# Order of the weight loads and place of one job's one-hots in the expert part of a transformer block

## The chip, the cores and the metric

The kernel runs on one core of one Trainium2 chip. The metric is device time in microseconds of one execution. The engines are named as in the profile: PE (TensorE, with PEld its weight loads), DVE (VectorE), ACT (ScalarE), POOL (GpSimd) and SP (SyncE, used here only to issue DMAs). Each engine takes its instructions in program order. A DMA is issued by an instruction on SP, ACT or POOL, and moves its data on the core's 16 DMA engines.

## The reference, cut to what matters

Sixteen sequences of 256 tokens with 256 features pass an attention layer with 16 heads. Then each of 8 experts chooses 512 of all 4096 tokens by their gate, and a two-layer network of that expert is added to those tokens.

```python
tok = x.reshape(-1, d)                      # after attention, 4096 x 256
gate = jax.nn.softmax(tok @ Wgate.T, axis=-1)
vals, idx = jax.lax.top_k(gate.T, k_cap)    # 512 tokens for each of 8 experts
idx_flat = idx.T.reshape(-1)
w = vals.T
g = _ln(tok[idx_flat], mlp_g, mlp_b).reshape(k_cap, E, d)
y = jnp.einsum('ked,ehd->keh', g, fc1s) + b1s       # hidden 1024
y = jax.nn.gelu(y, approximate=True)
y = jnp.einsum('keh,edh->ked', y, fc2s) + b2s
y = y * w[..., None]
tok = tok.at[idx_flat].add(y.reshape(-1, d))
```

## The kernel before

**Two ways of ordering.** The sequences are worked through first, under a plan written out by hand: each step of each part (a group of the projection, a quarter of the heads, a tail) has a number for its place, `at` collects the steps with their numbers, and one loop at L1064 issues them in the order of the numbers. A number is a place in the order and no time of this run. The tail of a sequence (`Tail`, two halves of 128 tokens each) projects the attention's result, adds the input (`residual`, which also writes the tokens to `out`), normalises (`power`, `apply`, which writes rows to `xn_dram`), transposes (`transposes`, `evict`) and computes the gate logits (`gate`, `gate_evict`). In the lists called `tail` the numbers stand in the order of these eight steps, `evict` sixth.

**Routing.** A first routing (`Routing`) chooses half of each expert's tokens, 256, from the first 30 tiles of 128 tokens, while the last sequence is still worked on; a second one chooses the other half from all 32 tiles. The second routing is cut into small steps that run inside the expert jobs (`second_routing`, L1074).

**Jobs.** There are 16 expert jobs (`Job`): eight of the first routing, numbered 0 to 7, and eight of the second, 8 to 15. A job
- loads its weights (`load`, L866): `w1` for the first layer (256 rows of 4 KB, L869), `w2` for the second (1024 rows of 1 KB, L871), and the bias `b2` (L873), all on SP;
- turns the routing into a list of tokens: `gives` (3 DVE operations, L879 and L887), one-hot matrices for each tile of tokens (`onehot`, L897, one DVE operation each), and a small matmul for each of these (`list_matmul`, L906); `take` brings the result to SBUF;
- fetches the chosen rows from `xn_dram` by two indirect DMAs of 128 rows on POOL (`gather`, L925) and transposes them (`transposes` L934, `evict` L941);
- runs the first layer (`up` L953 on PE, `gelu` L960 on ACT, eight of each) and the second (`down` L969, two halves of 128 tokens);
- finishes each half on DVE (`finish` L975, L976) and adds it to `out` by an indirect DMA on POOL (`scatter` L979). A scatter waits until the one before it has landed.

**Order in the jobs.** Job 0 and the lists of jobs 0 and 1 are part of the plan. Jobs 1 to 15 run in a loop (L1099) of 16 slots each: a slot is one `up` and `gelu` (slots 0 to 7) or a quarter of a `down` (slots 8 to 15). In job k, the list of job k+1 is multiplied and its rows are gathered at slot 5 (slot 7 in job 7), and they are transposed at slot 14. The one-hots of job k+2 are made a few at a time from slot 6 on (`lay_out`, `parts`), and at the end of job k job k+2's `load` is issued. For job 2, whose `load` follows the plan directly, `gives` and 18 one-hots come after the whole plan and the remaining 12 in the first slots of job 1.

**Buffers.** The tiles `v`, `oT` and `kT` of the attention have two buffers each and serve the jobs too: `w1` lies in `v`, `w2` in `oT`, the one-hots in `kT`. So `w1` of job k+2 can be written when job k's last `up` has read its `w1`, and `w2` when its last `down` has read its `w2`. SP issues in order: a load that must wait holds up those behind it. The one-hots of job 2 lie where those of job 0 lay.

The gates of the last two tiles of tokens also pass between: `Gates.shift` and `divide` (DVE, L718 and L725) and `exp` (ACT, L722) are issued in the first slots of job 1, and `parts` (POOL, L737) after them. ACT's gelu and exp use different tables, so a table is loaded at each change.

Of the kernel before, what the change touches and what calls it, by code (L numbers as in the profile page):

```python
# [9 lines left out]
F32 = mybir.dt.float32  # L10
# [8 lines left out]
P = 128  # L19
B, N, D = 16, 256, 256  # L20
# [5 lines left out]
NT = NTOK // P  # L26
# [3 lines left out]
FC = DD // P  # L30
# [13 lines left out]
def kernel(  # L44
# [14 lines left out]
    nc = tc.nc  # L59
# [20 lines left out]
    def rsqrt(dst, src):  # L80
# [99 lines left out]
        tail=((75.94, 79.63, 83.54, 87.30, 84.99, 86.37, 88.80, 89.54), (90.54, 94.23, 95.33, 101.91, 95.74, 99.41, 105.55, 106.29)),  # L180
# [71 lines left out]
    END = {  # L252
        13: dict(
            tail=((785.465, 790.273, 798.692, 815.100, 809.231, 833.838, 858.249, 860.611), (801.111, 811.928, 832.334, 851.976, 852.521, 857.274, 860.648, 863.953)),
        ),
        14: dict(
            quad={
                (0, 0): (778.689, 786.219, 823.152),
                (0, 0, 0): (779.682, 781.429, 786.791, 815.299, 818.486),
                (0, 0, 1): (785.912, 785.925, 792.535, 808.580, 817.952),  # L260
# [23 lines left out]
            tail=((862.946, 865.847, 868.980, 875.067, 865.880, 866.612, 872.508, 873.385), (858.831, 861.745, 877.140, 877.177, 862.888, 865.191, 867.264, 869.065)),  # L284
# [43 lines left out]
            tail=((961.580, 961.705, 961.951, 972.971, 962.994, 969.038, 969.773, 970.133), (961.977, 963.425, 970.214, 973.543, 969.153, 973.476, 975.274, 976.692)),  # L328
# [45 lines left out]
    if True:  # L374
        attw = ctx.enter_context(tc.tile_pool(name="attw", bufs=1))
        seq = ctx.enter_context(tc.tile_pool(name="seq", bufs=2))
# [368 lines left out]
        class Routing:  # L745
# [46 lines left out]
            def step(self, n):  # L792

                old, self.cand = self.cand, bit.tile([P, 1], I32, tag="cand", name="cand")
                nc.vector.scalar_tensor_tensor(
                    self.cand, self.dropped, (1 << n) >> 1, old,
                    ALU.bitwise_or, ALU.bitwise_xor,
                )
# [62 lines left out]
        class Job:  # L861
# [2 lines left out]
                self.oh = None  # L864

            def load(self):  # L866
                e = self.e
                self.w1 = seq.tile([P, DC, DD], F32, tag="v", name="w1")
                nc.sync.dma_start(self.w1, fc1T[e].rearrange("(c p) f -> p c f", p=P))  # L869
                self.w2 = seq.tile([P, FC, D], F32, tag="oT", name="w2")  # L870
                nc.sync.dma_start(self.w2, fc2T[e].rearrange("(f p) d -> p f d", p=P))  # L871
                self.b2 = moe.tile([P, D], F32, tag="b2", bufs=3, name="b2")
                nc.sync.dma_start(self.b2, b2s[:, bass.ts(e, D)].to_broadcast([P, D]))  # L873

# [113 lines left out]
        def at(places, *steps):  # L988
            plan.extend((p, len(plan) + n, f) for n, (p, f) in enumerate(zip(places, steps)))
# [60 lines left out]
        jobs = [Job(e, r, n) for r, n in ((first, n1), (second, NT)) for e in range(E)]  # L1050
# [10 lines left out]
        for i in range(KL):  # L1061
            at(DOWN[i], partial(jobs[0].down, i), partial(jobs[0].finish, i))
            at([SCATTER + i * 0.1], partial(jobs[0].scatter, i))
        for _, _, step in sorted(plan, key=lambda s: s[:2]):  # L1064
            step()

# [19 lines left out]
        def lay_out(job):  # L1086

            job.gives()
            for a in list(range(0, 18, 2)) + list(range(18, NT, 3)):
                yield  # L1090
                job.onehot(a, a + (2 if a < 18 else 3))
# [1 line left out]
        rest = second_routing()  # L1093
        last = len(jobs) // 2 - 2
        jobs[2].load()
        parts = lay_out(jobs[2])
        for _ in range(10):
            next(parts)
        for k in range(1, len(jobs)):  # L1099
            a = jobs[k]  # L1100
            new = jobs[k + 1] if k + 1 < len(jobs) else None
# [2 lines left out]
            for s in range(SLOTS):  # L1104
# [17 lines left out]
                if far and k != last and s > LIST_AT:  # L1122
                    if s == LIST_AT + 1:
                        parts = lay_out(far)
# [62 lines left out]
```

## Time and profile before

| | us |
|---|---|
| median of three runs | 1217.5 (1215.92 to 1219.42) |
| the profiled execution, its own time | 1216.65 |
| span of the profiled execution, first to last instruction | 1214.6 |
| PE busy | 1171.7 (96%) |
| DVE busy | 764.5 (63%) |
| ACT busy | 618.2 (51%) |
| POOL busy | 591.0 (49%) |
| issue to landing, median: `w1` and `w2` (1 MB each) | 5.3 and 5.4 |
| issue to landing, median: gather and scatter (128 KB each) | 3.3 and 3.9 |

The profile is taken from one execution, and its microseconds count from the first instruction. A busy time is that of an engine with an instruction in hand, so a high share says which engine to look at first and not that it wastes nothing. The page cuts the span into 40 slices of 30.4 us and gives the busy share of each in tenths. A row of the timeline has the start, the length, engine, source line and operation, the tiles written and read, the number of merged instructions, and in brackets how long the engine stood idle before it and what it then waited for. The lines of the kernel are those in this row (L934 is line 934).

### The profile page before, as it was taken

The numbers are of one execution on the slowest core, as the hardware profiler recorded it, in microseconds if no ns is written. First come the engines' busy times: TensorE is split into PE (matmuls) and PEld (weight loads), VectorE is DVE, ScalarE is ACT, GpSimd is POOL, SyncE is SP. The second block draws the span as 40 slices with busy tenths as digits, with TensorE's granted clock in tenths as the row PEclk, the third lists the DMA queues.
The fourth block names the chain that finished last, engine by engine and source line by source line (L and its number), as shares of the span: only waits on it lengthen the run. The fifth ranks groups of instructions, "written<-read, shape, count | busy, mean of one in ns | idle before, by whom it ended". The sixth has DMA issues, their size and how long they took to land. (4 is left out here: it accounts for less than half of the span.)

```text
span 1214.6 us, 19466 instructions
## 1 busy us (share of the span) xinstructions
PE 1171.7 (96%) x6784; PEld 813.2 (67%) x6784; DVE 764.5 (63%) x2244; ACT 618.2 (51%) x1701; POOL 591.0 (49%) x818
## 2 busy tenths in 40 slices
PE   6999999999999999999999999999978999999996
PEld 3556666666575766666666757667645788888885
DVE  7656665756665666666675666565587477864541
ACT  2655555555555555555555556656563233233331
POOL 4654555545455565455554545554564233333332
PEclk9999999999999999999999999999998999999999
DMA  5000000000000000000000000000200556665661
GB/s 183 1 1 5 22 8 20 9 18 14 14 14 14 27 2 26 5 22 10 18 10 18 14 14 19 9 19 13 97 0 2 176 154 178 182 182 164 165 179 23
DMA packets 46738, 62.40 MB, mean 51 GB/s; under 512 B 3888, under 2 KB 39984, under 8 KB 46640
## 3 DMA queue, kind: packets, MB, share of 16 engines
q1 hardware_dynamic: 39808, 52.70, 13.1%
q0 software_dynamic: 6144, 8.39, 3.8%
q8 instruction: 54, 0.88, 0.3%
q14 instruction: 44, 0.36, 0.1%
q10 hardware_dynamic: 688, 0.06, 0.0%
HBM read 48.56 MB, written 12.58 MB: 50 GB/s over the span
## 5 line engine op out<-in xcount | busy, mean ns | idle before, releaser
L608 POOL TENSOR_SCALAR pr<-pr,sums 128x256 f32<-128x256 f32 x512 | 238.7, 484 | 274.9 <-DVE sums L604 258.3
L506 PE MATMUL pm<-wq,hT 128*128 128x512 f32 x768 | 354.3, 600 | 5.5 <-DMA wq<-in_wqkvT 3.4
L597 ACT ACTIVATE pr<-sc,nmax 128x256 f32<-128x256 f32 x512 | 236.4, 476 | 161.7 <-DVE nmax L588 147.2
L82 POOL TENSOR_TENSOR ss<-ss,neghalf 128x8 f32<-128x8 f32 x128 | 210.4, 1648 | 97.1 <-DVE ss L527 93.4
L506 PEld LDWEIGHTS pm<-wq,hT 128*128 128x128 f32 x768 | 137.1, 191 | 148.0 <-issue 136.6
L588 DVE TENSOR_REDUCE nmax<-sc 128x2 f32<-128x512 f32 x256 | 164.7, 682 | 44.6 <-PE sc L581 44.4
L523 DVE TENSOR_REDUCE ss<-sq 128x8 f32<-128x512 f32 x128 | 87.4, 683 | 106.0 <-ACT sq L519 105.8
L617 PEld LDWEIGHTS pp<-ident,pr 128*128 128x128 f32 x1024 | 120.0, 144 | 35.0 <-issue 20.4
L617 PE MATMUL pp<-ident,pr 128*128 128x128 f32 x1024 | 140.0, 277 | 3.3 <-ACT pr L597 2.5
L635 PE MATMUL po<-prT,v 128*64 128x256 f32 x1024 | 139.4, 395 | 0.7 <-ACT oT L645 0.7
L581 PE MATMUL sc<-kT,qT 64*128 64x256 f32 x1024 | 130.2, 392 | 0.0
L519 ACT ACTIVATE sq<-pm 128x512 f32<-128x512 f32 x128 | 77.1, 602 | 90.4 <-PE pm L506 88.7
L659 PE MATMUL pw<-wo,oT 128*128 128x256 f32 x512 | 118.5, 384 | 0.0
L953 PE MATMUL ph<-xT,w 128*128 128x256 f32 x512 | 118.3, 384 | 0.0
L581 PEld LDWEIGHTS sc<-kT,qT 64*128 64x128 f32 x1024 | 94.2, 187 | 34.7 <-issue 24.0
L969 PE MATMUL py<-w,hid 128*128 128x256 f32 x512 | 117.4, 382 | 0.0
L979 POOL DMA_INDIRECT out<-y,idx x32 | 51.4, 1605 | 124.2 <-DVE y L976 59.9
L597 ACT ACTIVATION_READ_ACCUMULATOR pr<-sc,nmax 128x1 f32 x512 | 105.8, 207 | 0.0
L659 PEld LDWEIGHTS pw<-wo,oT 128*128 128x128 f32 x512 | 95.7, 192 | 13.0 <-issue 0.8
L625 DVE COPY prT<-pp 128x512 f32<-128x512 f32 x112 | 76.9, 687 | 43.6 <-PE pp L617 42.7
L953 PEld LDWEIGHTS ph<-xT,w 128*128 128x128 f32 x512 | 94.9, 190 | 13.4 <-ACT xT L941 0.2
L969 PEld LDWEIGHTS py<-w,hid 128*128 128x128 f32 x512 | 94.9, 190 | 13.1
(118 smaller groups left out, 1267.0 us busy)
## 6 DMA issues: line engine op xcount, KB each, us to landing
w<-in_fc1T SPq DMA_DIRECT2D x16, 1024.0 KB, 5.3
w<-in_fc2T SPq DMA_DIRECT2D x16, 1024.0 KB, 5.4
xs<-in_x SPq DMA_DIRECT2D x16, 256.0 KB, 2.7
out<-tok SPq DMA_DIRECT2D x32, 128.0 KB, 1.7
xn_dram<-tn SPq DMA_DIRECT2D x32, 128.0 KB, 1.7
wq<-in_wqkvT SPq DMA_DIRECT2D x6, 512.0 KB, 8.5
b<-in_b2s SPq DMA_DIRECT2D x16, 128.0 KB, 5.3
wo<-in_woutT SPq DMA_DIRECT2D x1, 1024.0 KB, 10.2
```

The source lines that it names most:

```text
L82: nc.gpsimd.tensor_tensor(dst, src, neghalf[:, : src.shape[1]], ALU.pow)
L506: nc.tensor.matmul(self.pm, hTs[self.b][:, c, bass.ts(self.t, P)], wq[:, c, bass.ts(self.g, GW)], start=(c == 0), stop=(c == DC - 1),)
L523: nc.vector.tensor_reduce(self.ss[:, 0, :], self.sq.rearrange("p (h d) -> p h d", d=HD), AX.X, ALU.add,)
L581: nc.tensor.matmul(self.sc[i, j][:, t, :], qTs[self.b][rows, hp, bass.ts(t, P)], kTs[self.b][rows, hp, :], start=True, stop=True,)
L588: nc.vector.tensor_reduce(self.nmax[i, j], self.sc[i, j], AX.X, ALU.max, negate=True)
L597: nc.scalar.activation(self.pr[i, j][:, t, :], self.sc[i, j][:, t, :], AF.Exp, bias=self.nmax[i, j][:, t : t + 1], scale=1.0, accum_out=se ...
L608: nc.gpsimd.tensor_scalar(self.pr[i, j][:, t, :], self.pr[i, j][:, t, :], self.sums[i][:, 1, j, t : t + 1], 1.0, ALU.mult, ALU.mult,)
L617: nc.tensor.transpose(self.pp[i, j][:, c, bass.ts(t, P)], self.pr[i, j][:, t, bass.ts(c, P)], ident,)
L635: nc.tensor.matmul(self.po[j * HD : (j + 1) * HD, i, :], vs[self.b][:, c, bass.ts(4 * self.d + 2 * i + j, HD)], self.prT[i, j][:, c, :], s ...
L659: nc.tensor.matmul(self.pw, oTs[self.b][:, hp, bass.ts(self.t, P)], wo[:, hp, :], start=(hp == 0), stop=(hp == HP - 1),)
L953: nc.tensor.matmul(self.ph[f], self.w1[:, c, bass.ts(f, P)], self.xT[:, c, :], start=(c == 0), stop=(c == DC - 1),)
L969: nc.tensor.matmul(self.py[i], self.hid[:, f, bass.ts(i, P)], self.w2[:, f, :], start=(f == 0), stop=(f == FC - 1),)
```

## The change

Two things are changed. In `load`, `w2` is allocated and requested before `w1`. And for job 2, `gives` and all 30 one-hots are put into the plan at the place of the `evict` of the last sequence's first tail (the smaller sixth number of the two in `END[15]["tail"]`, 969.038, behind that `evict` as it was entered earlier); `parts` is empty until job 1 begins those of job 3.

```diff
             def load(self):
                 e = self.e
+                self.w2 = seq.tile([P, FC, D], F32, tag="oT", name="w2")
+                nc.sync.dma_start(self.w2, fc2T[e].rearrange("(f p) d -> p f d", p=P))
                 self.w1 = seq.tile([P, DC, DD], F32, tag="v", name="w1")
                 nc.sync.dma_start(self.w1, fc1T[e].rearrange("(c p) f -> p c f", p=P))
-                self.w2 = seq.tile([P, FC, D], F32, tag="oT", name="w2")
-                nc.sync.dma_start(self.w2, fc2T[e].rearrange("(f p) d -> p f d", p=P))
                 self.b2 = moe.tile([P, D], F32, tag="b2", bufs=3, name="b2")
                 nc.sync.dma_start(self.b2, b2s[:, bass.ts(e, D)].to_broadcast([P, D]))
...
             at(DOWN[i], partial(jobs[0].down, i), partial(jobs[0].finish, i))
             at([SCATTER + i * 0.1], partial(jobs[0].scatter, i))
+        at([min(t[5] for t in END[B - 1]["tail"])] * 2, jobs[2].gives,
+           partial(jobs[2].onehot, 0, NT))
         for _, _, step in sorted(plan, key=lambda s: s[:2]):
             step()
...
         jobs[2].load()
-        parts = lay_out(jobs[2])
-        for _ in range(10):
-            next(parts)
+        parts = iter(())
         for k in range(1, len(jobs)):
```

## The prediction, made before the changed kernel was run

> **What bounds the kernel now.** I read the page's slices first, then busy time by stage, then TensorE's own timeline through the expert jobs, then the DMA issues of one job.
>
> ```profile
> PE   6999999999999999999999999999978999999996
> DMA  5000000000000000000000000000200556665661
> q1 hardware_dynamic: 39808, 52.70, 13.1%
> ```
>
> TensorE (PE) is the bound almost everywhere; DMA is idle until the expert jobs, and there it is busy 60% of the time. The change only touches these jobs (from about 950 us) and the last tail before them. By stage (columns: stretch, its length, busy us and instructions of PE, weight loads, DVE, ACT, POOL, clock, DMA share, GB/s):
>
> ```profile
> 967.20:985.50 18.30, 17.38 (x103) 14.41 (x102) 14.24 (x77) 7.26 (x13) 8.12 (x10) 1.00 0.56 155
> 985.50:1080.20 94.70, 94.56 (x624) 80.70 (x623) 72.05 (x366) 28.84 (x60) 31.30 (x24) 1.00 0.61 176
> 1080.20:1175.70 95.50, 92.21 (x602) 79.82 (x601) 48.38 (x252) 28.84 (x60) 31.13 (x24) 1.00 0.61 174
> 1175.70:1190.80 15.10, 15.10 (x101) 13.31 (x100) 4.25 (x21) 4.80 (x10) 5.18 (x4) 1.00 0.39 108
> ```
>
> These are job 1, jobs 2 to 7, jobs 8 to 13 and job 14. Job 14 does what jobs 8 to 13 do, in 15.1 us instead of 15.9; the difference between them is that no weights are fetched during its middle. Where the others lose it, PE's timeline shows (start, length, idle before and releaser); job 14 comes last:
>
> ```profile
> 1093.19 0.27 PE L934 MATMUL px<-ident,xg 128*128 128x128 f32 x1
> 1094.13 0.55 PE L934 MATMUL px<-ident,xg 128*128 128x128 f32 x3 [0.67 <-DMA xg<-xn_dram,idx]
> 1094.51 1.89 PE L969 MATMUL py<-w,hid 128*128 128x256 f32 x8
> ...
> 1188.64 0.60 PE L934 MATMUL px<-ident,xg 128*128 128x128 f32 x4
> 1189.08 1.89 PE L969 MATMUL py<-w,hid 128*128 128x256 f32 x8
> ```
>
> The transposes of the next job's gathered rows take 0.44 us from their start to the next matmul in job 14, and 1.32 in job 8: the second gather is late. Its competitor, from SP's and POOL's timelines and the landing times of the gathers of job 8, then job 14 (min/median/max):
>
> ```profile
> 1088.20 0.37 SPq L869 DMA_DIRECT2D w<-in_fc1T  x1
> 1087.98 0.98 POOL L925 DMA_INDIRECT xg<-xn_dram,idx  x1 [0.30 <-issue]
> DMA to landing us min/median/max: 2.8/4.5/6.1
> DMA to landing us min/median/max: 2.8/2.8/2.9
> ```
>
> The first-layer weights w1 are let go when the job's eighth `up` is done, so their load starts within 0.2 us of the second gather, which then takes 6.1 us instead of 2.9 and lands at 1094.1, when w1 lands (issue to landing 5.7).
>
> [...] a gather issued among twenty one-hots at 943.46 took 1.25 us, its neighbour at 945.00, still among them, 0.97. [...] the trace shows 1.28 before and after the gates' exp in job 1.
>
> **Part 1, the loads.** With w2 first in SP's queue, w2 waits for the old job's last `down`, and w1, which could have gone 8 us earlier, stands behind it. Nothing else is queued on SP then except b2 and later loads. Count from a job's first `up`, T (job 8: 1080.21). Before: w2 at T+0.2, data until T+5.8, DMA empty until T+8, w1 at T+8.0, data until T+13. After: w2 at T+0.2, w1 at about T+0.6, b2 behind. The second megabyte at the 366 to 434 GB/s of the full one-microsecond slices costs 2.4 to 2.9 us, so w1 is in by about T+8.5 and the weights by T+9 at worst. They are needed at T+15.8: cover of 7 us. The gathers start at T+6.45 and T+7.8. The first meets the last microsecond of w1, the second is nearly alone: 2.9 us, landing at T+10.7, or T+11.7 if delayed one more. PE comes to the transposes at T+13.0. The stall goes, and PE's own work is next.
>
> The sum: jobs 8 to 13 take 16.03, 16.04, 15.83, 15.89, 15.61 and 16.06 us from first `up` to first `up`, job 14 takes 15.14. The excesses are 0.89, 0.90, 0.69, 0.75, 0.47 and 0.92, together 4.6. Job 7's transposes start 0.31 late and take 0.12 too long: 0.4. Jobs 2 to 6 hardly stall (0.17 at 1014.70), as their list comes at T+4.5 and the second gather has a lead: 0.2. Part 1 in jobs 2 to 13: 5.2 us.
>
> The scatter of the old job's second half, at T+1.3, now lies beside two loads. It took 4.1 to 5.3 us beside one, 7.1 once (1177.0). The next scatter, at T+12.5, waits for it, so it has cover until then: nothing.
>
> Job 1's own load (issued 949.04 and 949.53) swaps order. w2 must await the last projection, which ends at 949.31, so the pair ends 0.3 later, and job 1's gathers, already starved to the pair's end (5.5 and 6.3 us), with them. PE waits there at 958.45. Bounds: 0.5 gained[...] to 1.0 lost. I take 0.2 lost. The `out` and `xn_dram` writes behind the load on SP shift by as much, with no reader near.
>
> **Part 2, the one-hots.** They are not removed: 3 DVE operations of `gives` and 30 one-hots go from after job 0's finish to after the first tail's `evict`. That one ends on DVE at 952.12, and the next DVE instruction waits until 959.96:
>
> ```profile
> 951.71 0.41 DVE L687 COPY tokT<-pg 128x256 f32<-128x256 f32 x1
> 959.96 0.17 DVE L698 COPY gates<-pl 128x8 f32<-128x8 f32 x1 [7.84 <-PE pl L692]
> ...
> 968.85 3.05 DVE L897 TENSOR_SCALAR oh<-lane,partf 128x128 bf16<-128x128 bf16 x18
> 972.40 0.91 PEld L906 LDWEIGHTS <-oh 128*128 128x128 bf16 x6 [0.36 <-DVE oh L897]
> 974.75 1.11 PE L953 MATMUL ph<-xT,w 128*128 128x256 f32 x4
> ```
>
> Eighteen take 3.05 us, twenty 3.40 to 3.59 elsewhere, so 30 take 5.1 to 5.4; `gives` takes 0.71 (968.14 to 968.85). The block ends at 957.9 to 958.2 in a hole that ends at 959.96: free, with 1.8 us to spare. Their tile is that of job 0's one-hots, last read at 942.76, so no new wait. Behind the block on DVE stand the gate copy, `choose`, the second tail's `evict` and `apply`; if the hole were short, PE's gate matmul (963.31) still has another 1.7 us after that `evict` (961.45). POOL issues job 1's gathers at 952.00 and 953.31 beside the block: 0 to 0.3 us, of which half is in the 0.2 above.
>
> What it frees: DVE goes from the finish (968.2) straight to the gates' `shift`, ACT's exp comes at 970.05 when its table is in, instead of 972.21, and the second gelu at 971.6 instead of 973.74. PE's list at 971.53 finds all 30 one-hots and takes 0.76 (as in job 2, 990.10 to 990.86), so the sixth `up` comes at 972.3 instead of 974.75: 2.45 us. Not all of it arrives. The next gathers stand on POOL behind scatter, scatter, casts: the second scatter (974.05) waits for the first one's landing, and the gathers at 977.19 and 978.54 do not come sooner. PE would want them at 980.5. Without w1 beside them (977.84 before) they land at 978.54 + 2.9 = 981.4 instead of about 983.4. But the first scatter now flies beside two loads: 0 to 1.8 us later (5.3 there, 7.1 at worst), and the gathers with it. So job 1 gains 2.0 to 0.2; I take 1.2.
>
> **Sum**: 5.2 + 1.2 - 0.2 = 6.2 us. The profiled execution took 1216.65 (span 1214.6 and 2 us around it), giving 1210.4. The median of the three times is 0.85 above it, so 1217.5 - 6.2 = 1211.3.
>
> **Rivals.** (a) Forecast, 1211.3: chance 0.70. The time is 1208.5 to 1213.8 within it. (b) Only the loads pay: POOL's chain eats job 1's gain, and the early gathers lose 1 us. For it: at 974.05 POOL has waited 3.81 us for the first scatter's landing, so that landing sets all that follows. Gain 5.2 + 0.2 - 1.0 = 4.4, time 1213.1; chance 0.09. (c) Gathers still collide: if the two loads last until T+11, the second gather is held to about T+12 to T+13.2 and keeps half of the stall; with job 1's gain lost, 2.6, so 1214.9, no change to be told. [...] Against: 360 to 434 GB/s in every full slice. Chance 0.12. (d) Slower: the stream of 2 MB outlasts the gather in every job. Price: at the slowest load seen (w2 at 1175.86, 7.3 us to landing) two in a row end at T+0.2+14.6 = T+14.8, and the transposes wait 1.8 us in each of jobs 1 to 13: 23.4 added, 5.4 of old stalls gone, 1235.5. It decides once the stream ends after T+13.4 (at that point each job waits 0.4, as now on average). Against: 5.0 to 5.6 us for all other loads[...]. Chance 0.09, which holds milder forms also.
>
> **Numbers.** The range of 1208.0 to 1215.6 takes in both ends of job 1's gain, the early gathers, and (c). A measurement of this kernel can tell about 0.3% from no change, 3.7 us here, that is below 1213.8 or above 1221.2. Faster: (a) and most of (b), 0.78. Same: (c) and the rest, 0.13. Slower: (d), 0.09.
>
> **What would show it.** w2 and w1 issued 0.4 us apart just after T, nothing at T+8; gather landings near 2.9 to 3.9 us; job lengths of jobs 8 to 13 near 15.15; no DMA idle ahead of their transposes; thirty one-hots between 952 and 958.3, with the gate copy still at about 960; the sixth `up` of job 1 about 5.1 us after its first. Wrong: gathers landing after T+13, the gate copy late behind the one-hots, or scatters that land so late that they hold POOL when the gathers are due.

## The result and the profile after

The changed kernel takes 1214.63 us (median of 20 runs, 1212.41 to 1217.34) against 1218.43 for the kernel before in the same sessions (20 runs). The ratio is 0.9967 with a 95% interval of 0.9957 to 0.9978: faster by 4.0 us, from 2.7 to 5.2. The forecast was 6.2.

In the changed kernel the lines after the head of `load` stand two lower on the page (`onehot` L899, `transposes` L936, `up` L955, `down` L971, `scatter` L981). The profiled execution took 1212.76 us with a span of 1210.8. By stage (columns as before; job 0 from its first `up`, job 1, jobs 2 to 6, job 7, jobs 8 to 13, job 14):

```profile
949.40:966.30 16.90, 15.93 (x82) 13.64 (x79) 9.71 (x50) 6.19 (x12) 2.61 (x3) 1.00 0.49 172
966.30:986.90 20.60, 17.49 (x103) 14.89 (x102) 8.83 (x44) 7.26 (x13) 8.17 (x10) 0.92 0.51 141
986.90:1065.50 78.60, 78.60 (x523) 67.24 (x523) 60.49 (x303) 24.03 (x50) 26.05 (x20) 1.00 0.59 175
1065.50:1081.00 15.50, 15.50 (x103) 13.55 (x102) 11.63 (x63) 4.81 (x10) 5.21 (x4) 1.00 0.62 179
1081.00:1171.80 90.80, 90.80 (x601) 80.06 (x600) 48.58 (x252) 28.85 (x60) 31.28 (x24) 1.00 0.62 183
1171.80:1187.00 15.20, 15.20 (x102) 13.38 (x102) 4.25 (x21) 4.81 (x10) 5.18 (x4) 1.00 0.62 183
```

Jobs 8 to 13 have PE busy without a gap. Job 1 has grown from 18.3 to 20.6 us, and its mean clock is 0.92.

The lengths from first `up` to first `up`, read from PE's timeline in each trace:

| | before | changed |
|---|---|---|
| job 0 | 16.64 | 16.87 |
| job 1 | 18.35 | 20.63 |
| jobs 2 to 6 | 78.80 | 78.63 |
| job 7 | 15.85 | 15.43 |
| jobs 8 to 13 | 95.46 | 90.85 |
| job 14 | 15.14 | 15.14 |
| from job 0's first `up` to the end of the span | 264.03 | 261.37 |

So in these two traces, one execution of each kernel, the part from the first `up` on is 2.66 us shorter. The other 1.1 us of the spans' difference lie ahead of the first `up` (950.57 and 949.43), where the kernels differ only in the order of the loads of jobs 0 and 1, requested from 867.6 and 948.2 on in the changed one. Between 890 and 950 us PE often waits (busy 47.4 of the 60 us before, 47.3 in the changed kernel) and its mean granted clock differs from run to run (0.86 before, 0.89 in the changed kernel, 0.81 with the split load below), and this point moved between 949.4 and 954.6 in the traces of this study. The job lengths below are free of that.

Where job 1 loses its time, from PE's timeline of the changed kernel, and below the dots the same place before:

```profile
970.62 0.90 PE L908 MATMUL pls<-give,oh 128*128 128x10 bf16 x30
971.37 1.11 PE L955 MATMUL ph<-xT,w 128*128 128x256 f32 x4
...
981.91 0.30 PE L936 MATMUL px<-ident,xg 128*128 128x128 f32 x1 [2.17 <-DMA xg<-xn_dram,idx]
983.14 0.90 PE L936 MATMUL px<-ident,xg 128*128 128x128 f32 x3 [0.93 <-DMA xg<-xn_dram,idx]
983.84 3.25 PE L971 MATMUL py<-w,hid 128*128 128x256 f32 x8
986.93 1.03 PE L955 MATMUL ph<-xT,w 128*128 128x256 f32 x4
...
982.97 0.31 PE L934 MATMUL px<-ident,xg 128*128 128x128 f32 x1
983.45 0.55 PE L934 MATMUL px<-ident,xg 128*128 128x128 f32 x3 [0.17 <-DMA xg<-xn_dram,idx]
983.83 1.89 PE L969 MATMUL py<-w,hid 128*128 128x256 f32 x8
985.56 1.03 PE L953 MATMUL ph<-xT,w 128*128 128x256 f32 x4
```

All 30 list matmuls run in one go and the sixth `up` comes 5.07 us after the first, as forecast. Then PE stands for 3.1 us before the transposes of job 2's rows, and the eight `down` matmuls behind them take 3.09 us until the next `up`, instead of 1.73. POOL's timeline shows why the rows are late; the last three lines are from before:

```profile
967.61 1.67 POOL L981 DMA_INDIRECT out<-y,idx  x1 [13.80 <-DVE gates L719]
975.68 1.57 POOL L981 DMA_INDIRECT out<-y,idx  x1 [6.41 <-DMA out<-y,idx]
976.70 0.78 POOL L737 CAST vals<-gate_of 128x16 bf16<-128x16 f32 x1
...
978.83 1.15 POOL L927 DMA_INDIRECT xg<-xn_dram,idx  x1
980.28 0.99 POOL L927 DMA_INDIRECT xg<-xn_dram,idx  x1 [0.30 <-issue]
...
968.52 1.73 POOL L979 DMA_INDIRECT out<-y,idx  x1 [13.65 <-DVE chunk L879]
974.05 1.57 POOL L979 DMA_INDIRECT out<-y,idx  x1 [3.81 <-DMA out<-y,idx]
977.19 1.04 POOL L925 DMA_INDIRECT xg<-xn_dram,idx  x1
```

In the changed kernel job 0's first scatter is issued at 967.61. The second one waits 6.41 us for it to land, the casts of the last gates stand behind that, and job 2's gathers behind the casts. The time from issue to landing of that first scatter, before and changed, and then of the two gathers in the changed kernel:

```profile
DMA to landing us min/median/max: 5.3/5.3/5.3
DMA to landing us min/median/max: 7.8/7.8/7.8
...
DMA to landing us min/median/max: 2.8/2.9/2.9
```

The gathers themselves are quick. The scatter took 5.3 us before and takes 7.8 now, beside two weight loads instead of one.

### The profile page after: what moved, and what is told of

Read it like the earlier page. It is cut to its first block, busy times and chain, and to the rows that moved or that the text cites. A ratio compares the mean times of both kernels' runs of the same rounds, so it can differ in the third digit from the quotient of the medians.

```text
span 1210.8 us, 19463 instructions
## 1 busy us (share of the span) xinstructions
PE 1168.7 (97%) x6784; PEld 813.0 (67%) x6784; DVE 764.4 (63%) x2244; ACT 618.2 (51%) x1701; POOL 591.3 (49%) x818
## 5 line engine op out<-in xcount | busy, mean ns | idle before, releaser
L617 PEld LDWEIGHTS pp<-ident,pr 128*128 128x128 f32 x1024 | 118.3, 143 | 34.9 <-issue 19.6
L971 PE MATMUL py<-w,hid 128*128 128x256 f32 x512 | 118.7, 385 | 0.0
L955 PE MATMUL ph<-xT,w 128*128 128x256 f32 x512 | 118.3, 384 | 0.0
L981 POOL DMA_INDIRECT out<-y,idx x32 | 51.4, 1606 | 125.2 <-DVE y L978 61.9
L971 PEld LDWEIGHTS py<-w,hid 128*128 128x128 f32 x512 | 96.0, 192 | 13.5
L955 PEld LDWEIGHTS ph<-xT,w 128*128 128x128 f32 x512 | 94.9, 190 | 13.4 <-ACT xT L943 0.2
```

Source lines behind the costliest of these rows:

```text
L617: nc.tensor.transpose(self.pp[i, j][:, c, bass.ts(t, P)], self.pr[i, j][:, t, bass.ts(c, P)], ident,)
L955: nc.tensor.matmul(self.ph[f], self.w1[:, c, bass.ts(f, P)], self.xT[:, c, :], start=(c == 0), stop=(c == DC - 1),)
L971: nc.tensor.matmul(self.py[i], self.hid[:, f, bass.ts(i, P)], self.w2[:, f, :], start=(f == 0), stop=(f == FC - 1),)
```

## Experiments

Two explanations were set against each other. Theory 1: POOL's chain, as just read, with the second load beside the scatter as its cause. Theory 2: the moved one-hots cost job 1 its time themselves. The first four kernels ran in one session (before: 1218.49 us), the other three in a second one on another chip (before: 1217.85 us). The job lengths are those of one profiled execution of each kernel. The edits are shown against the changed kernel.

**The loads alone.** The new order in `load`; the one-hots of job 2 where they were.

```diff
-        at([min(t[5] for t in END[B - 1]["tail"])] * 2, jobs[2].gives,
-           partial(jobs[2].onehot, 0, NT))
...
-        parts = iter(())
+        parts = lay_out(jobs[2])
+        for _ in range(10):
+            next(parts)
```

> The new order of the loads alone; job 2's one-hots where they were. Theory 1 (POOL's chain: job 0's first scatter flies beside 2 MB, the second scatter waits for its landing, job 2's gathers stand behind it): that scatter still lands about 7.8 us after its issue and the gathers come as late as in the changed kernel, but PE reaches the transposes 2.5 us later and so waits only about 1 us there: job 1 takes about 19 us (18.35 before, 20.63 changed), jobs 8 to 13 take 15.14 each. Time about 4.3 us below before, that is 1 to 2 us below the changed kernel. Theory 2 (the moved one-hots themselves cost job 1 its time): job 1 at 17.9 or less, and the time 2.7 us or more below the changed kernel.

Measured: 1212.89 us, ratio 0.9963 (0.9950 to 0.9976). Job 1 takes 19.29 us, jobs 8 to 13 take 90.85 together. The first scatter lands after 7.8 us without any one-hot moved, which speaks for theory 1. But PE did not wait for the gathers at all; the excess of 0.9 over 18.35 came from another place:

```profile
973.45 1.00 PE L906 MATMUL pls<-give,oh 128*128 128x10 bf16 x6 [0.47 <-DVE oh L897]
974.31 2.05 PE L953 MATMUL ph<-xT,w 128*128 128x256 f32 x4
```

Four `up` matmuls took twice their 1.1 us. The windows of this trace give a clock of 0.50 from 974.3 to 976.8, so the wait for one-hots was followed by a slow stretch, which the expectation had not counted. The second gather landed at 983.6, 0.3 us before PE came to the transposes (983.88). From the sixth `up` to the first `down` 4.25 us had passed, 1.35 more than before; without these PE would have waited about 1 us, as expected (an estimate from these times). The expected total, 4.3 below before, came out (4.5) because the slow stretch took the place of the wait, which is luck. The rest of the time forecast, 1 to 2 us below the changed kernel, is not shown: the ratios are 0.9963 here and 0.9967 there.

**The one-hots alone.** The changed kernel with the two loads in the old order.

```diff
-                self.w2 = seq.tile([P, FC, D], F32, tag="oT", name="w2")
-                nc.sync.dma_start(self.w2, fc2T[e].rearrange("(f p) d -> p f d", p=P))
                 self.w1 = seq.tile([P, DC, DD], F32, tag="v", name="w1")
                 nc.sync.dma_start(self.w1, fc1T[e].rearrange("(c p) f -> p c f", p=P))
+                self.w2 = seq.tile([P, FC, D], F32, tag="oT", name="w2")
+                nc.sync.dma_start(self.w2, fc2T[e].rearrange("(f p) d -> p f d", p=P))
```

> The one-hots moved alone; loads in the old order. Theory 1: the first scatter of job 0 flies beside w2 alone and lands after about 5.3 us, the sixth up of job 1 comes 5.1 us after the first, but PE then meets job 2's gathers, which still fly beside job 3's w1: a wait of 2 to 3 us at the transposes, job 1 at 18.2 to 19.6 us, so nothing gained: the time is from 0 to 1.2 us above before. Theory 2: the same wait or a longer one without any late scatter, job 1 at about 20.6.

Measured: 1215.68 us, ratio 0.9980 (0.9970 to 0.9989), and job 1 at 16.61 us. Both theories' numbers for job 1 missed (18.2 to 19.6 and about 20.6), and so did theory 1's for the time, 0 to 1.2 us above before where it is 2.4 below. The scatter landed after 5.2 us, as theory 1 had it, but PE waited only 0.77 us for job 2's rows:

```profile
980.16 0.30 PE L936 MATMUL px<-ident,xg 128*128 128x128 f32 x1 [0.61 <-DMA xg<-xn_dram,idx]
980.62 0.55 PE L936 MATMUL px<-ident,xg 128*128 128x128 f32 x3 [0.16 <-DMA xg<-xn_dram,idx]
```

Job 1's `up`s ended earlier, so job 3's w1 was asked for earlier too (974.29, where it was 977.84). The gathers (976.06 and 977.42) flew beside it, but the DMA traffic of this stretch was over by 980 (342 GB/s from 978 to 980, 35 from 980 to 982), so the rows came soon after PE asked for them. Theory 2 falls here: without the new load order the moved one-hots shorten job 1 by 1.7 us.

**The changed kernel, with job 2's load in the old order.** Only `jobs[2].load` asks for w1 first.

```diff
-            def load(self):
+            def load(self, old=False):
                 e = self.e
-                self.w2 = seq.tile([P, FC, D], F32, tag="oT", name="w2")
-                nc.sync.dma_start(self.w2, fc2T[e].rearrange("(f p) d -> p f d", p=P))
+                if not old:
+                    self.w2 = seq.tile([P, FC, D], F32, tag="oT", name="w2")
+                    nc.sync.dma_start(self.w2, fc2T[e].rearrange("(f p) d -> p f d", p=P))
                 self.w1 = seq.tile([P, DC, DD], F32, tag="v", name="w1")
                 nc.sync.dma_start(self.w1, fc1T[e].rearrange("(c p) f -> p c f", p=P))
+                if old:
+                    self.w2 = seq.tile([P, FC, D], F32, tag="oT", name="w2")
+                    nc.sync.dma_start(self.w2, fc2T[e].rearrange("(f p) d -> p f d", p=P))
...
-        jobs[2].load()
+        jobs[2].load(True)
```

> The changed kernel, with w1 before w2 for job 2's load alone. Theory 1: w1 is fetched at about 961 us, only w2 flies beside the first scatter, which lands after about 5.3 us; job 2's gathers come 2.5 us sooner and PE waits about 1 us instead of 3.1 for them, without the half clock after: job 1 at about 16.6 us, the time about 4 us below the changed kernel. Theory 2: job 1 stays at 20.6 and the time stays at the changed kernel's.

Measured: 1210.80 us, ratio 0.9942 (0.9921 to 0.9962). Job 1 takes 16.36 us, with w1 asked for at 962.50 and the scatter landing after 5.3 us. From POOL's and PE's timelines:

```profile
974.40 1.60 POOL L983 DMA_INDIRECT out<-y,idx  x1 [3.92 <-DMA out<-y,idx]
...
981.76 0.55 PE L938 MATMUL px<-ident,xg 128*128 128x128 f32 x3 [0.63 <-DMA xg<-xn_dram,idx]
```

One swap in one load is worth 4.3 us in job 1, the wait and the slow clock behind it together: theory 1 holds, and the whole loss is in this load.

**Job 0's second scatter behind job 2's gathers.** The loads as changed, so the first scatter still flies beside both.

```diff
-            at([SCATTER + i * 0.1], partial(jobs[0].scatter, i))
+            if i == 0:
+                at([SCATTER], partial(jobs[0].scatter, i))
...
                     new.gather()
+                    if k == 1:
+                        jobs[0].scatter(1)
```

> The changed kernel, with job 0's second scatter issued behind job 2's gathers on POOL; loads and one-hots as changed. Theory 1: the first scatter still takes 7 to 8 us, but the gathers go at about T+6 and T+7.3, beside the loads until about T+9.5, and land by T+11, before PE wants them at T+13.3: no wait, clock 1.0, job 1 at 15.6 us, the time about 5 us below the changed kernel. If the loads' traffic itself, and not the place on POOL, held the gathers, they would land at T+15 or later and job 1 stay above 18. Theory 2: job 1 stays at 20.6.

Measured: 1209.14 us, ratio 0.9931 (0.9909 to 0.9953), job 1 at 15.50 us, with the clock at 1.00 throughout. POOL's and PE's timelines:

```profile
973.17 1.16 POOL L927 DMA_INDIRECT xg<-xn_dram,idx  x1 [0.75 <-DVE chunk L881]
974.63 0.96 POOL L927 DMA_INDIRECT xg<-xn_dram,idx  x1 [0.30 <-issue]
976.65 1.64 POOL L981 DMA_INDIRECT out<-y,idx  x1 [1.05 <-DMA out<-y,idx]
...
980.57 0.64 PE L936 MATMUL px<-ident,xg 128*128 128x128 f32 x4
981.04 1.89 PE L971 MATMUL py<-w,hid 128*128 128x256 f32 x8
```

The gathers go 5.9 us after job 1's first `up` instead of 12.5, beside the loads' last part, and PE finds the rows there. The second scatter now waits behind them (1.05 us) for the first one. The loads' traffic is not what held the gathers: it was their place behind a scatter that waits.

**The same without the moved one-hots.** To see what part 2 is worth when POOL is out of the way. On top of the edit just shown:

```diff
-        at([min(t[5] for t in END[B - 1]["tail"])] * 2, jobs[2].gives,
-           partial(jobs[2].onehot, 0, NT))
...
-        parts = iter(())
+        parts = lay_out(jobs[2])
+        for _ in range(10):
+            next(parts)
```

> The new order of the loads and job 0's second scatter behind job 2's gathers, with job 2's one-hots where they were before. If the moved one-hots are worth what the prediction gave them (2.45 us) as soon as POOL no longer holds the gathers, job 1 takes 15.5 + 2.45 = 17.95 us here and the time lies about 2.4 us above late_scatter. If they are worth nothing, job 1 takes 15.5 and the times agree.

Measured: 1212.80 us, ratio 0.9959 (0.9947 to 0.9972), and job 1 at 19.52 us, 4.0 more than with the moved one-hots. That is 1.6 more than expected: the clock is 0.50 from 976 to 978 and below 1.00 on both sides, again after PE's waits in the list. So in these traces the moved one-hots are worth about 2.3 us (2.45 forecast) and a slow stretch of about 1.7.

**Job 1's load split.** On top of the later scatter alone, job 1 asks for w1 at its old place in the plan, and for w2 and b2 after the plan.

```diff
-        at(LOAD, jobs[0].load, jobs[1].load)
+        at(LOAD, jobs[0].load, jobs[1].load1)
...
+        jobs[1].load(a=False)
         jobs[2].load()
```

`load1` holds the two lines for `w1`; `load(a=False)` does the rest.

> late_scatter with job 1's load split: w1 at its place in the plan, w2 and b2 only after the plan, ahead of job 2's load. If job 1's gathers are late because 2 MB fly beside them, they now land about 3 to 4 us after their issue, PE no longer waits at the first transposes, and job 0 takes about 15.8 us from its first up to job 1's instead of 16.84; the time lies about 1 us below late_scatter. If they are late for another reason, job 0 stays at 16.8.

Measured: 1208.60 us, ratio 0.9921 (0.9908 to 0.9934), the fastest of all, 9.6 us below before by the ratio. Job 0 takes 15.49 us, 1.35 less than with the later scatter, and the second gather of job 1's rows lands after 2.8 us instead of 5.6. PE's row for job 1's rows has no wait any more:

```profile
954.62 7.20 PE L958 MATMUL ph<-xT,w 128*128 128x256 f32 x32
961.65 0.60 PE L939 MATMUL px<-ident,xg 128*128 128x128 f32 x4
```

The 0.5 us between the medians of the two kernels (in two sessions) is less than the 1.35 us in the trace, and their intervals overlap, so the times do not show this gain. The traces do: job 0 took 16.48 to 17.29 us in the eight others.

**The changed kernel again.**

> The changed kernel once more, for job 1 and the clock in it. If the halved clock after PE's wait is a regular price of that wait, job 1 takes 20.6 us again with three microseconds at half clock; if it comes and goes, job 1 takes about 19.3 us at full clock. PE waits 3 us at the transposes either way.

Measured: 1215.62 us, ratio 0.9980 (0.9970 to 0.9991). PE waits 3.4 us at the transposes, the scatter landed after 8.1 us, and job 1 takes 21.29 us. Windows of this trace, cut where its clock changes:

```profile
982.13:985.54 3.41, 0.88 (x5) 0.41 (x3) 1.99 (x12) 0.00 (x0) 2.73 (x3) 1.00 0.22 58
985.54:988.96 3.42, 2.51 (x8) 2.15 (x9) 0.00 (x0) 1.02 (x2) 0.95 (x1) 0.50 0.39 59
988.96:992.37 3.41, 3.41 (x11) 2.51 (x9) 1.28 (x5) 0.00 (x0) 0.47 (x1) 0.50 0.13 34
```

So the halved clock came back, this time for 6.8 us and into job 2 (16.57 us instead of 15.67). In both traces of the changed kernel it comes with the wait; whether it does so in every run was not seen. Why the two measurements of one kernel differ (0.9967 and 0.9980, intervals that overlap a little) was not pursued.

## Why the prediction was right, and where it was off

The direction was right and the time lies in the range; the gain was 4.0 us where 6.2 were forecast. The time itself, 1214.63, is outside the 1208.5 to 1213.8 that the forecast's own line (a) allowed. About 1 us of that is the kernel before, which took 1218.43 here and 1217.5 in the three runs from which the forecast started.

**The loads, jobs 2 to 13: 5.2 forecast, 5.20 measured** (4.61 in jobs 8 to 13, 0.42 in job 7, 0.17 in jobs 2 to 6). In job 8 w1 is asked for 0.66 us after the first `up`, T, and lands 8.0 us later, at T+8.6. The gathers, issued at T+6.5 and T+7.8, land after 3.0 and 2.7 us. In jobs 8 to 13 the second gather takes 2.7 to 3.5 us now and took 5.7 to 6.1 before. In job 8 it now has w1 beside it for its first 0.9 us only, where before w1 was asked for 0.22 us after it. That it is late beside a whole load is measured (6.1 us there, 2.7 now); how queues share the DMA engines is not shown. The two sums agree so closely because the forecast added up the stalls of this same trace of before. Stalls differ between executions: with the one-hots alone, whose loads are in the old order, jobs 8 to 13 took 94.00 us and not 95.46, and jobs 2 to 6 took 78.63, so their 0.17 is not owed to the loads.

**Job 1's own load: 0.2 lost forecast, 0.23 measured** as job 0's length. That the order of the load is the reason is not shown: job 0 took 16.48 and 16.61 us in the two kernels with the new order and the one-hots in their old place, 16.63 with the one-hots alone, and 16.84 to 17.29 in the four that have both. The split load shows that 1.35 us can be had there.

**The one-hots: free, and they are.** DVE's timeline of the changed kernel:

```profile
951.61 5.05 DVE L899 TENSOR_SCALAR oh<-lane,partf 128x128 bf16<-128x128 bf16 x30
...
959.04 0.17 DVE L698 COPY gates<-pl 128x8 f32<-128x8 f32 x1 [2.38 <-PE pl L692]
```

They end 2.4 us ahead of the gate copy. The gathers that POOL issued beside `gives` and the one-hots (950.86 and 952.17) took 1.00 and 0.96 us, as before (1.00 and 0.95), so the block cost their issue nothing here. ACT's table loads on both sides of the gates' exp in job 1 took 1.28 us each in both traces.

**Job 1: 1.2 us gained forecast, 2.3 lost.** This is nearly the whole difference between 6.2 and 2.66 in the traces. The failed term is the one for POOL's chain, "the first scatter now flies beside two loads: 0 to 1.8 us later (5.3 there, 7.1 at worst), and the gathers with it". The chain was named rightly, its place too, but the scatter took 7.8 and 8.1 us in the two traces of the changed kernel: 2.5 to 2.8 later, beyond the worst that the trace of before had shown. That worst was of scatters beside one load (4.1 to 6.0 us there, and 7.1 once; the prediction's "4.1 to 5.3" is too narrow), and no scatter beside two had been seen. It is no freak of job 0: the thirteen later scatters beside two loads took 6.9 to 8.2 us in the changed kernel, and no later scatter had to wait for them, as the prediction had said. From the issue of job 0's first scatter to the first gather 11.2 us pass instead of 8.7. PE, which now came 2.5 us sooner, waited 3.1 us. The next matmul of `down` follows at T+17.54, where it came at T+16.62; of these 0.92 us, 0.32 are three transposes at a lower clock (0.70 us to the next matmul instead of 0.38). So the late rows make job 1 about 0.6 us longer than before. The other 1.7 us are the clock, for which the sum had no term at all: 0.32 in the transposes and 1.36 in the eight matmuls behind them.

**The two parts together.** In job 1, from 18.35 us, the one-hots alone take off 1.7, the loads alone add 0.9, both add 2.3. They are not additive: the one-hots bring PE to the transposes sooner, the loads bring the rows later, and a half-clock stretch came with the loads alone and with both, but not with the one-hots alone. With the scatter moved, both together take off 2.85.

**The rivals.** (b) named the right mechanism, POOL's chain eating job 1's gain, but left job 1 0.2 us of gain where 2.3 were lost, and gave the early gathers 1 us where 0.23 were lost; that its 4.4 lies near the measured 4.0 is luck. (c) had nearly the measured sum in the trace, 2.6, for a reason that did not happen: no gather of jobs 8 to 13 came late for PE. (d) did not come: in job 8 the two loads ended 4 us before PE needed the rows (T+8.6 and T+13.0).

## What to carry to other kernels

When a load is moved out of the way of one transfer, list what it flies beside in its new place, and follow each of those to what waits for its landing; here a scatter on another queue was held (7.8 us to landing instead of 5.3), and a gather stood behind its successor, which waited 6.41 us. Work that nothing waits for (a second scatter) belongs behind work that the bound engine needs soon (the gather) where it would stand waiting ahead of it: behind the gathers it left job 1 at 15.50 us, ahead of them at 20.63. Where two edits shorten and lengthen the two sides of one wait, price them together.

## What was not expected of the hardware

In the profiled execution of the changed kernel a wait of PE cost more than its length: with the 3.1 us of job 1 came 3.41 us at a clock of 0.50. Its windows (columns as in the stages above), cut where its clock changes, have the wait of job 1 in the first and half the clock in the second:

```profile
979.75:983.17 3.42, 0.33 (x2) 0.17 (x2) 1.53 (x9) 0.00 (x0) 2.81 (x3) 1.00 0.27 77
983.17:986.58 3.41, 3.41 (x10) 2.87 (x11) 0.00 (x0) 1.02 (x2) 0.04 (x1) 0.50 0.35 38
986.58:989.99 3.41, 3.41 (x18) 2.93 (x17) 2.76 (x15) 1.11 (x3) 1.57 (x1) 1.00 0.47 119
```

The lengths of such stretches repeat: in the traces of before and of the changed kernel each half-clock stretch that ends within the span lasts 3.41, 6.83 or 10.24 us, and the one in the second trace of the changed kernel, above, 6.83. With PE at work throughout, 3.41 us at a clock of 0.50 cost about 1.7 us, half their length (an estimate from these two figures; 0.32 and 1.36 were read above).

Half clock came also where PE had mostly been at work. The first line below is the list stage of the loads alone, with PE busy for 2.67 us of 3.41; behind it the clock was 0.50. The other two are the same stage before the change, in steps of 3.41 us from the clock's last change at 945.84 (that such steps matter is the author's assumption). PE was busy for 3.15 and 2.93 us of them, and the clock stayed at 1.00:

```profile
970.25:973.66 3.41, 2.67 (x31) 1.90 (x29) 3.31 (x23) 1.83 (x3) 0.00 (x0) 1.00 1.05 383
...
969.73:973.15 3.42, 3.15 (x33) 2.46 (x31) 3.38 (x24) 1.24 (x3) 0.52 (x1) 1.00 1.04 311
973.15:976.56 3.41, 2.93 (x17) 2.27 (x17) 2.95 (x18) 2.62 (x6) 2.28 (x5) 1.00 0.16 10
```

Divided so, the small matmuls and the waits of the stage fall mostly into one piece in the first trace, and in the other they are divided between two. That this made the difference is the author's estimate. What decides it is not shown: PE's busy time in such a piece does not decide it alone, as 2.02 us of 3.41 were followed by full clock in another place (958.24 to 961.65 in the second trace of the changed kernel).

An accumulating scatter of 128 rows landed after 3.7 to 3.8 us with nothing beside it (job 14), after 4.1 to 6.0 beside one load of 1 MB (7.1 once), and after 6.9 to 8.2 beside two.
